# Cross attention on one core: an earlier x load, six warm-up products instead of 14, a last product in two halves, and a new order at both ends

## The chip, the cores and the metric

The kernel runs on one core of one Trainium2 chip. The metric is the device time of one execution in microseconds (us), the median of several runs. Beside it there is the trace of one execution, taken by the hardware profiler. Its engines are PE (TensorE matmuls; PEld are its weight loads), DVE (VectorE), ACT (ScalarE), POOL (GpSimd) and SP (SyncE, which here only issues DMA transfers).

## The reference

x has shape (2, 2048, 640), the text (2, 128, 384). The last four text rows (`ca`) are treated apart from the first 124 (`enc`). Cut to what matters, with eight heads of 80:

```python
enc, ca = text[:, :124, :], text[:, 124:, :]
hs = mha(x @ Wq, enc @ Wk, enc @ Wv)              # x attends to the text
ca_q1 = einsum('btc,th->bch', ca, Wq_ca)[:, indices, :]   # 2048 rows out of 384
ca_hs1 = mha(ca_q1, x, x)                         # the four rows attend to x
ca_hs2 = mha(ca_hs1 @ Wq, ca @ Wk_ca, ca @ Wv_ca)
out = (hs + ca_hs2) @ Wout + b_out + x
```

`mha` is softmax(q k^T / sqrt(80)) v for each head. All of it is float32.

## The kernel before, in words

The kernel is a set of generators, each of which hands out its steps one at a time. Every step names its engine, the steps it comes after, the rooms (PSUM banks, buffers) it takes and frees, and the marks it sets. `Desk.run` walks through the table `ORDER`. Each entry is the number of a task, whose next step is issued there; a letter behind it chooses ACT (`a`), DVE (`v`) or POOL (`g`) where a step may run on several engines. What is issued is pinned, so that each engine works strictly in the order of the table. The tile framework adds the waits. All DMA transfers that matter here are issued by SP, in the table's order, and a transfer waits for the one eight places ahead of it, since there are eight DMA semaphores.

The work is done in three stretches.

- **The front.** `first_loads` fetches four tiles of 128 rows of x (`xz`, one for each `row(k)`) and Wq in five chunks of rows (`wq_rows(c)`, into `wq_sb`), then Wq_ca, the text (`ctx_sb`), Wk_ca (`w_kca`), Wk (`w_k`) and further x rows (`xi`). `idle_work` multiplies a tile of zeros with itself (PSUM tile `unread`, helper `warm`); nothing reads the result. `x_first` transposes the first rows of x (`pt_x_0` to `pt_x_4`); `context` transposes the text (`pt_ctx_0` to `pt_ctx_2`), from which `ctxT`, `caT` and `cadT` are copied. `queries` forms the first queries (`pq_first`) chunk by chunk of x's columns, as chunks of Wq arrive. `y_weights` multiplies `w_kca` with `cadT` (`p2_kca`; the profile prints `p_kca`), and makes from it and from a turned Wq (`wq_turned`, `pt_wq_c_0` and `pt_wq_c_4`, c = 0 to 4) the weights `wyz` of the products `pyz`. `keys` makes `pk`, `text_values` the values `pv_b_u` of the two texts (24 matrix multiplies of 320 columns on the trace for a pair `b_u`).
- **The middle.** For 16 units of two tiles of 128 rows: queries (`pq`), scores against the text (`sc`), exponentials (`p`), products with values (`ph`, evacuated to `hs`), and for the four text rows the scores against x (`s1_...`, four multiplies of 512 columns into one PSUM tile of 2048), the maximum of each (`mx`, on DVE) and their exponentials. The tiles `s1_...` share PSUM room, so that a later one waits for the `mx` of an earlier one.
- **The end.** `text_out_fast` makes the output product `hs @ Wout` of a unit in seven products on sums and differences of blocks, whose partial results DVE adds in halves of 320 columns to x's rows, already in `x_more` or `last_rows`. The chains of partial products are run by `sums_chain`, with `po_m_...` the PSUM tile of unit m (`HALF` is 320). `stored` issues the store of a finished piece; in unit 15 a piece is half a row tile of 128, 128x320.

On PE the helper `matmul` cuts a product with 128 columns of weights into four strips of 32, each with its own weight load, so that a product is one row of the order and several rows of the trace. The profile's lines L211, L215, L219, L226 and L236 are the helpers for products, zeros, transposes, engine operations and transfers.

Of the kernel before, what the change touches and what calls it, by code (L numbers as in the profile page):

```python
# [66 lines left out]
class Desk:  # L67
# [7 lines left out]
        2 2 2 2 2 2 36 0 0 0 4 4 0 0 0 0 0 0 0 0 4 0 0 111a 6 6 6 0 4 6 4 2 2 2 2 2 2 2 4 113a 107 108 109 110 4 6  # L75
        114a 115a 3 6 3a 3 116v 4 6 3a 3 3v 6 3 8 8 7 7 7 2 15 15 15 11 15 15 12 8 7 0 0 118a 8 5 15 15 15 15 10 7
        117a 15 7 8 7 7 7 120a 9 1 119v 8 6 121a 7 7 7 7 122a 7 7 124v 9 123v 125a 126a 8 8 127 8 9 8 36 5 128 8 8 8 5
        9 9 9 129 5 130 15 36 15 15 131 9 9 14 14 9 14 14 14 14 9 14 6 112 136a 133a 135v 134v 14g 137 36 112 11 112
        15 14 15 36 14 12 14g 36 138 138 138 36 138 138 12 12 12 36 144v 145v 12 36 36 11a 9 9 9 139 11 9 9 9 140 143a
        9 146a 12 13 101 17 106 140 140 140 140 141 18 6 140 140 140 140 142 106 132 132 16 17 147g 148g 132 101v 142  # L80
        132 101v 101g 101g 101g 39 152 152 152 152 152 152 151 17 17 36 36 156a 142 142 142 18 18 18 18 18 18 18 18
        132 142 16 151 152 36 36 142 16 16 157a 43 151 152g 149g 152 16 132 16 101v 101 18 16 16g 36 159 159 16 36 158
        36 101g 150g 101g 17 160a 159 159 16 151 161a 16g 155 18 18 18 152 162 36 153 36 18 158 158 18 158 155 17 155
        153 36 20 20 19 163 159 159 163 163 21 21 171 163 142 142 158 172 164 163 163 36 21 21 172 172 172 172 21 43
        154 36 154 175 175 165 159 36 175 175 175 175 19 19 19 159g 166g 167g 159 36 36 170 39 181a 36 170 21 21 21 21
        172 172 172 19 20 19 19 182 177 176 177 182 175 19g 19 177 177 159 173 36 20 183a 170 20 36 168g 182 182 182
        182 172 19 184a 20 178 170 178 182 169g 175g 17 21 21 21 21 21 21 22 19g 177 174 177 185 23 182g 36 36 185 185
        186a 185 185 175 24 24 24 24 24 175 24 174 174 24 24 188 24 174 187 185 36 22 47 22 22 22 192 22 180 194 179
        36 180 192 192 192 192 22 192 22g 182 190 174 182 36 179 180 36 195 192 196 36 47 174 174 174 158 20 23 202 23
        23 24 24 24 197 22 197 198g 192g 199v 36 192 36 24 201g 24 206a 197 197 197 22 200g 197 23 202 23 208 51 207a  # L90
        208 174 189 208 208 208 208 197 197g 22g 36 209 209 36 202 205 209 214a 209 192 132 197 189 158 189 189 189
        197 132 189 202 36 215a 209 205 189 209 36 216 55 36 203 205 209 217 217 24 209g 36 26 26 217 217 217 217 209
        217 27 27 27 27 27 158 209 210 27 212 27 204 36 204 203 218 51 36 36 225 224 219g 220g 222g 221g 217g 36 193
        226 226 223 228 230a 223 228 36 226 226 226 226 232a 229 193 217 132 158 217 158 189 23 189 191 191 191 191 27
        55 231v 36 36 233v 229 223 226 193 193 193 234 234 226g 36 226 235 234 234 234 234 25 26 229 234 36 236 36 36
        27 191 226 191 191 191 191 27 211 36 227 223 227 237 27 238 234g 234 25 59 239 239 25 25 27 27 27 27 239 239
        239 239 36 211 36 211 132 211 211 177 36 26 59 26 36g 241 241 211 211 211 211 213 29 29 241 241 241 247 239
        243v 240 251v 25 36 36 36 26 244g 247 36 252 252 254a 36 247 36 252 252 30 234 213 56 177 30 30 30 30 213 213
        213 25 239g 241 241 239 239 240 177 245g 241g 242 249 36 36 252 253 252 255a 253 247 249 253 253 36 253 36 25
        256v 253 36 63 252 193 252 252 40 213 28 252 36 44 30 30 30 30 193 262 262 257 246g 240 241 250 263 241 177 25  # L100
        240 213 262 262 262 262 36 67 36 36 252 213 240 30 30 30 264 30 264 30 250 252 250 36 30 262 265 262g 262 264
        264 213 36 252 252 31 252 29 31 36 252 264 264 31 36 67 36 31 193 193 258 260 193 262 259 259 10 259 36 60 26
        33 33 33 33 252 252 252 29 36 29 252 29 32 268 32 31 33 267 267 33 33 259 266 266 259 264 264g 269g 270g 264
        266 266 36 266 266 268 36 36 268 268 268 63 252 266 252 252 252 252 276 268 276 266v 267 31 33 264 267 274 273
        276 276 252 282a 36 36 36 252 273 36 283 283 284v 273 36 276 276 36 36 283 283 248 36 248 259 242 259 259 283
        283 271g 272v 276 31 242 285v 273 36 36 31 267 32 259 31 283 36 283 266 286 287v 33 31 283 28 36 31 28 28 36
        31v 252 28 283 281 71 36 283 276v 289 283 281 261 261 261 261 261 261 25 28 266 277 28 261 36 290 33 283 290
        288 33 36 281 283 290 290 36 290 290 33 291 33 276 33 33 32 36 75 28 25 276 25 36 261 283 28 35 35 68 283 283
        290 25v 292 292 290g 242 242 290 292 292 292 261 292 25 25 32 32 275 298 292 36 298 283 36 283 34 293v 294g
        25v 298 298 75 36 292g 298 298 301 295g 301 290 292 36 280 242 280 242 275 275 275 292 302 288 275 28 301 301  # L110
        301 301 28 28g 301 304 279 242 71 279 242 242 305 306 242 305 305 305 305 305 297 103 35 242 283 35 242 242
        283 283 307 288 242 102 275 68 296g 66 66 31 31 31g 36 36 275 275 275 299 68 68 28 11 310v 301v 307 35 242 64
        314 29 283 314 283 28 35 315 301 314 28g 316 283 48 283 283 309 317a 242 242 297 309 283 313 242 313 318a 313
        242 314 314 309 313 297 316 316 305 242 242 288 288 301 10 305g 32 316 278 278 278 316 313a 320a 308 297 308
        316 305 242 323 319 242 324 242 34 34 34 34 313 325 68 68 68 105 103 104 104 267 48 79 242 332 242 48 48 34 46
        46 278 34 321 34 278 305 332 311g 328g 330g 329g 68 68 335a 68 242 336a 331g 312g 339g 340g 333g 341g 338g 34
        102 105 40 38 38 34 48 48 40 48 278 68 288 337a 332 332 332 332 79 242 344 242 348 332 344 242 346 348 346 344
        344 242 242 345 344 242 344 344 348 278 348 34 348 278 278 348 52 332g 332 347 344 242 345 83 242 349 349 242
        349 349 349 349 345 345 349 347 48 242 352a 48 48 48 334g 359 34g 242 242 300 44 300 34 332 40 40 40 44 44 40
        300 44 44 44 351 288 300 300 349g 355g 349 349 288 42 240 240 42 34 354a 353a 356g 34g 357g 343g 358g 342g 242  # L120
        360 83 242 360 360 365 359 365 242 365 365 365 365 359 359 362 362 365 242 361 359 242 242 300 104 361 360 359
        242 40 359 40 44 242 359 365g 363g 40 367a 300 40 300 369a 368a 300 372g 365 373g 371a 87 348 242 380 380 44
        242 242 242 381a 44 384v 374v 380 382a 380 380 52 44 242 242 242 380 364g 385g 375g 376 376 378 377 387 378
        387 376 387 387 376 379 387 376 379 288 240 50 52 288 52 240 242 52 242 52 242 242v 242 366 240 365 52 50 377
        380 380g 348g 393g 392g 327 387 376 242 377 387 376 242 242 242 391 303 303 303 303 303 380 377 376 327 267
        387 327 327 380 267 391 52 52 242 391 391 242 52 52 327 391 60 327 396v 397v 403 303 303 386v 383v 403 399v
        400g 401v 242 398a 91 407 407 242 391 303 303 322 35 64 391 407 407 407 407 403 391 242 389 407 327 395 403
        403 403 242 242 242 391 322 327 267 322 267 322 322 327 402v 407g 407 407 391 403 404 242 389 403 242 91 64 60
        327 64 64 391 322 391 391 391 242 404 404 408 408 348 322 408 408 242 408 408 404 390 348 64 64 58 409 370 408
        390 242 242 95 411 411 388 388 408g 408 322 391 391 388 242 322 326 411 411 411 411 242 95 411 388 412 412 391  # L130
        391 391 64 414v 242 391 413 408 62 62 411g 411 411 64 412 412 242 412 412 405 242 242 417v 405 87 418 412 418
# [108 lines left out]
def kernel(  # L240
# [42 lines left out]

# [1877 lines left out]
```

## Time and profile before

| | |
|---|---|
| time, median of 3 runs | 565.43 us (565.28 to 566.68) |
| the profiled execution's own time | 563.94 us |
| its span in the trace | 562.1 us |
| PE busy | 554.3 us, 99% |
| DVE busy | 386.8 us, 69% |
| ACT busy | 265.5 us, 47% |
| POOL busy | 198.9 us, 35% |
| moved by DMA | 101.47 MB, mean 181 GB/s |
| PE on the chain that ended last | 92% |
| DVE on that chain | 6% |

The span runs from the first to the last instruction of the trace; 1.84 us of the execution's own time lie outside it. PE is busy in nearly the whole span, but busy is not the same as advancing: in the first microseconds each multiply takes about twice as long as later, and the multiplies of zeros count as busy. A row of the timeline gives the start of a group in us from the span's start, then its length, the engine, the line, the operation, the tiles, the shape and how many instructions it holds. Groups on PE overlap a little, since the end of a multiply is modelled; the distance from one row's start to the next row's is the better duration.

### The profile page before, as it was taken

Reading aid. Unit: us, or ns where it says so; the run is one execution under the profiler, and the core shown is the slowest. Engines: PE = TensorE matmul, PEld = TensorE weight load, DVE = VectorE, ACT = ScalarE, POOL = GpSimd, SP = SyncE. Lnnn points to the kernel's source line nnn. Section 1 sums busy time; section 2 is a strip of 40 time slices with the busy share of each in tenths; the row PEclk is TensorE's granted clock in tenths of the full one; section 3 lists DMA queues with packets and bytes.
Section 4 is the critical chain, followed back from the end, with each engine's and each line's share of the span. In section 5 each row is a group of like instructions: output and inputs, shape, how many; then the busy total and the mean of one; then the engine's idle time right before and its main releaser. Section 6 shows DMA issues by size and latency. Waiting matters only on the chain.

```text
span 562.1 us, 18792 instructions
## 1 busy us (share of the span) xinstructions
PE 554.3 (99%) x8064; PEld 313.9 (56%) x8064; DVE 386.8 (69%) x622; ACT 265.5 (47%) x732; POOL 198.9 (35%) x211
## 2 busy tenths in 40 slices
PE   9999999999999999999999999999999999999997
PEld 8564455556555655555465445455545666666664
DVE  1457999999996564579999998755635655555534
ACT  3123645445338898886525424589878130100100
POOL 7002625344424522013469364512330513321310
PEclk9999999999999999999999999999999999999999
DMA  8994859764877989456568795859853687688703
GB/s 263 241 173 127 168 114 162 165 158 142 175 194 157 182 250 180 130 168 175 172 134 254 214 235 134 243 160 256 254 161 111 179 188 190 153 255 231 210 24 141
DMA packets 151554, 101.47 MB, mean 181 GB/s; under 512 B 86476, under 2 KB 130012, under 8 KB 151472
## 3 DMA queue, kind: packets, MB, share of 16 engines
q1 hardware_dynamic: 150704, 99.88, 69.8%
q8 instruction: 63, 1.03, 0.8%
q0 software_dynamic: 768, 0.40, 0.4%
q14 instruction: 19, 0.16, 0.1%
HBM read 61.34 MB, written 38.90 MB: 178 GB/s over the span
## 4 chain that ended last, share of the span: by engine, by line
PE 92%; DVE 6%; issue 1%; ACT 1%; DVEq 0%; ACTq 0%
PE po L211 26%; PE pq L211 25%; PE acc L211 8%; PE sc L211 7%; PE s L211 7%; PE ph L211 7%; DVE mx L226 4%; PE pq_first L211 3%; PE pyz L211 3%; PE pk L211 1%; PE unread L215 1%; PE pv L211 1%; DVE m L226 1%; PE pt_wq L219 1%; PE pt_x L219 0%
## 5 line engine op out<-in xcount | busy, mean ns | idle before, releaser
L226 DVE TENSOR_REDUCE mx<-s 128x4 f32<-128x2048 f32 x48 | 109.3, 2277 | 2.9 <-PE s L211 2.7
L226 ACT ACTIVATE p<-sc,m 128x124 f32<-128x124 f32 x256 | 89.8, 374 | 32.9 <-DVE m L226 32.9
L226 ACT ACTIVATE ea<-s 128x2048 f32<-128x2048 f32 x48 | 90.4, 1884 | 25.6 <-PE s L211 25.4
L226 POOL TENSOR_TENSOR p<-p,r 128x992 f32<-128x992 f32 x28 | 52.0, 1858 | 133.1 <-DVE r L226 129.2
L211 PE MATMUL po<-wout_sums,hs 128*32 128x320 f32 (+1 forms) x1012 | 77.8, 433 | 0.5 <-DVE x_more L226 0.5
L211 PE MATMUL po<-wout_sb,hs 128*32 128x320 f32 x956 | 76.9, 433 | 0.0
L226 DVE TENSOR_TENSOR x_more<-x_more,po 128x320 f32<-128x320 f32 x72 | 33.7, 481 | 44.6 <-PE po L211 44.5
L226 ACT ACTIVATION_READ_ACCUMULATOR p<-sc,m 128x1 f32 x256 | 55.4, 216 | 0.0
L211 PE MATMUL pq<-xt,wq_sb 128*32 128x256 f32 x896 | 54.3, 381 | 0.6 <-DVE q L226 0.6
L211 PEld LDWEIGHTS po<-wout_sums,hs 128*32 128x32 f32 (+1 forms) x1012 | 37.6, 110 | 29.5 <-issue 1.4
L211 PEld LDWEIGHTS po<-wout_sb,hs 128*32 128x32 f32 x956 | 36.3, 111 | 27.5 <-issue 0.9
L211 PE MATMUL acc<-ea,y_sb 128*32 128x384 f32 (+2 forms) x768 | 50.4, 384 | 0.0
L226 DVE TENSOR_REDUCE m<-sc 128x4 f32<-128x496 f32 x64 | 40.8, 663 | 13.4 <-PE sc L211 13.4
L226 POOL TENSOR_TENSOR hs<-hs 128x256 f32<-128x256 f32 x35 | 27.6, 796 | 60.9 <-DVE hs L226 52.4
L211 PE MATMUL ph<-pT,vpad 128*32 128x256 f32 x768 | 46.7, 380 | 0.3 <-ACT p L226 0.3
L226 DVE STREAM_TRANSPOSE eb<-p 128x1024 f32<-128x1024 f32 x32 | 39.5, 1234 | 5.0 <-POOL p L226 3.2
L226 DVE TENSOR_TENSOR last_rows<-last_rows,po 128x320 f32<-128x320 f32 x56 | 26.2, 479 | 23.1 <-PE po L211 22.9
L211 PEld LDWEIGHTS pq<-xt,wq_sb 128*32 128x32 f32 x896 | 27.5, 110 | 22.9 <-issue 5.5
L226 ACT COPY hs<-ph 128x512 f32<-128x512 f32 (+1 forms) x23 | 12.2, 543 | 58.8 <-PE ph L211 58.6
L211 PE MATMUL pq<-xt,wq 128*32 128x512 f32 x320 | 38.8, 595 | 0.0
L211 PEld LDWEIGHTS sc<-kmain,q 64*128 64x128 f32 x512 | 31.9, 187 | 11.7 <-issue 8.2
L211 PE MATMUL sc<-kmain,q 64*128 64x124 f32 x512 | 37.6, 283 | 0.1
(197 smaller groups left out, 792.5 us busy)
## 6 DMA issues: line engine op xcount, KB each, us to landing
kept<-eb SPq DMA_DIRECT2D x32, 512.0 KB
pT<-kept SPq DMA_DIRECT2D x48, 256.0 KB
landing<-away SPq DMA_DIRECT2D x60, 128.0 KB
xi<-in_x_dram SPq DMA_DIRECT2D x28, 256.0 KB
x_more<-in_x_dram SPq DMA_DIRECT2D x18, 320.0 KB
out_dram<-x_more SPq DMA_DIRECT2D x18, 320.0 KB
last_rows<-in_x_dram SPq DMA_DIRECT2D x14, 320.0 KB
y<-yt SPq DMA_DIRECT2D x16, 256.0 KB
```

What stands on the lines that cost most here:

```text
L211: self.pin(self.nc.tensor.matmul(out[strip], lhsT[:, strip], rhs, **kw))
L215: self.pin(self.nc.tensor.matmul(out, zeros, zeros, start=True, stop=True))
L219: self.pin(self.nc.tensor.transpose(out, in_, ident))
L226: return lambda *args, **kw: self.pin(getattr(engine, what)(*args, **kw))
```

## The change

Four edits, and an order that goes with them.

1. `first_loads` issues the second tile of x ahead of Wq's first chunk.
2. `IDLE` goes from 14 products of zeros to 6. Before, nine came ahead of `pt_x_0`, three between `pt_x_0` and `pt_x_1` and two among the `pt_wq`. Now all six come ahead of `pt_x_0`, and the transposes of x come after the mark "zeros".
3. The last chain of unit 15, a product of 12 steps over 320 columns with one addition and one store, is made as two chains of 160 columns, each with its addition and its store.
4. `ORDER` is recorded anew. Of some 2,235 entries about the first 250 and the last 45 differ; between them only task numbers shift.

```diff
-    FAST, SPARE, IDLE = 1, 0, 14
+    FAST, SPARE, IDLE = 1, 0, 6
...
-        for op in (row(0), wq_rows(0), row(1), row(2), row(3)):
+        for op in (row(0), row(1), wq_rows(0), row(2), row(3)):
...
-            yield Do("PE", product, [] if n else [op.at], frees=[(banks, at)] if n == IDLE - 1 else [])
+            end = n == IDLE - 1
+            yield Do("PE", product, [] if n else [op.at], frees=[(banks, at)] if end else [], marks=["zeros"] if end else [])
...
-            op = yield Do("PE", turn, [("xrows", n)] if n < 4 else [("xlast", k) for k in range(4)], needs=[(banks, 1)])
+            op = yield Do("PE", turn, [("xrows", n), "zeros"] if n < 4 else [("xlast", k) for k in range(4)], needs=[(banks, 1)])
...
-        def sums_chain(m, n, steps):
+        def sums_chain(m, n, steps, c0=0, c1=HALF):
...
-                            to[:, :HALF], l, r, start=(k == 0 and c == 0), stop=(c == len(pairs) - 1),
+                            to[:, c0:c1], l, r[:, c0:c1], start=(k == 0 and c == 0), stop=(c == len(pairs) - 1),
...
         for n, steps in enumerate(chains):
-            yield Fork(sums_chain(m, n, steps))
+            if m < UNITS - 1 or n < 3:
+                yield Fork(sums_chain(m, n, steps))
+            else:
+                left["products"] += 1
+                yield Fork(sums_chain(m, n, steps, 0, HALF // 2))
+                yield Fork(sums_chain(m, n + 1, steps, HALF // 2, HALF))
...
+    spans = (0, HALF), (HALF, H), (0, H), (HALF, HALF + HALF // 2), (HALF + HALF // 2, H)
...
     ORDER = """
-        2 2 2 2 2 2 36 0 0 0 4 4 0 0 0 0 0 0 0 0 4 0 0 111a 6 6 6 0 4 6 4 2 2 2 2 2 2 2 4 113a 107 108 109 110 4 6
+        36 0 4 4 0 0 0 0 0 2 2 2 2 2 107 0 0 4 4 111v 112a 6 6 6 6 6 4 2 110 2 2 2 2 2 2 2 4 3 108 109 114v 4 1 3v 3
...
```

**PE, the front.** These rows of PE's order before stand from the second set of `pq_first` products over 512 columns (which needs Wq's third chunk, DMAHW0) to the transposes `pt_wq_1_0`; a name in brackets is the semaphore waited for.

```order
L211 MATMUL pq_first_0_197<-xt_0_0_179,wq_sb_98 128x512 [waits DMAHW0_49]
L211 MATMUL pq_first_1_198<-xt_0_0_179,wq_sb_98 128x512
L211 MATMUL pq_first_2_199<-xt_0_0_179,wq_sb_98 128x512
L211 MATMUL pq_first_3_200<-xt_0_0_179,wq_sb_98 128x512
L211 MATMUL p2_kca_284<-w_kca_226,cadT_124 32x160 [waits DMAHW7_49,DVE_49]
L211 MATMUL p2_kca_284<-w_kca_226,cadT_124 32x160 x11
L219 MATMUL pt_wq_0_0_300<-ident_69,wq_sb_98 128x128 [waits Activation_49]
L219 MATMUL pt_wq_0_0_300<-ident_69,wq_sb_98 128x128 x3
L219 MATMUL pt_wq_0_4_322<-ident_69,wq4_99 128x128 [waits DVE_49,PE_49]
L215 MATMUL unread_177<-zeros_158 128x128 x2
L219 MATMUL pt_wq_1_0_339<-ident_69,wq_sb_98 128x128 [waits DVE_49,PE_49]
L219 MATMUL pt_wq_1_0_339<-ident_69,wq_sb_98 128x128 x3
```

The same place after the change:

```order
L219 MATMUL pt_wq_0_0_283<-ident_69,wq_sb_98 128x128 x4
L211 MATMUL p2_kca_305<-w_kca_231,cadT_124 32x160 [waits DVE_49,DMAHW7_49,Activation_49,Pool_49]
L211 MATMUL p2_kca_305<-w_kca_231,cadT_124 32x160 x11
L219 MATMUL pt_wq_0_4_327<-ident_69,wq4_99 128x128 [waits Activation_49]
L219 MATMUL pt_wq_1_0_329<-ident_69,wq_sb_98 128x128 [waits PE_49]
L219 MATMUL pt_wq_1_0_329<-ident_69,wq_sb_98 128x128 x3
L211 MATMUL pq_first_0_200<-xt_0_0_171,wq_sb_98 128x512 [waits DMAHW0_49]
L211 MATMUL pq_first_1_201<-xt_0_0_171,wq_sb_98 128x512
L211 MATMUL pq_first_2_202<-xt_0_0_171,wq_sb_98 128x512
L211 MATMUL pq_first_3_203<-xt_0_0_171,wq_sb_98 128x512
```

`p2_kca`, which waits for the transfer of `w_kca` (DMAHW7), now stands ahead of that set of `pq_first`; the two products of zeros are gone from here.

**PE, the values and the first scores.** Before, the end of the front reads:

```order
L211 MATMUL pv_0_1_634<-w_v_315,ctxT_122 32x320 x12
L211 MATMUL pv_1_0_647<-w_v_315,ctxT_122 32x320 [waits DVE_49,PE_49]
L211 MATMUL pv_1_0_647<-w_v_315,ctxT_122 32x320 x11
L211 MATMUL s1_0_0_1_0_660<-zop_0_0_531,cop_153 128x512 [waits PE_49]
L211 MATMUL s1_0_0_1_0_660<-zop_0_0_531,cop_153 128x512 x3
L211 MATMUL pv_1_1_671<-w_v_315,ctxT_122 32x320 [waits DVE_49,PE_49]
L211 MATMUL pv_1_1_671<-w_v_315,ctxT_122 32x320 x11
L211 MATMUL s1_0_0_1_1_685<-zop_0_0_531,cop_153 128x512 [waits DVE_49]
L211 MATMUL s1_0_0_1_1_685<-zop_0_0_531,cop_153 128x512 x3
```

After the change:

```order
L211 MATMUL pv_0_1_618<-w_v_301,ctxT_122 32x320 x12
L211 MATMUL s1_0_0_1_0_651<-zop_0_0_522,cop_153 128x512 [waits DVE_49]
L211 MATMUL s1_0_0_1_0_651<-zop_0_0_522,cop_153 128x512 x3
L211 MATMUL pv_1_0_657<-w_v_301,ctxT_122 32x320 x12
L211 MATMUL pv_1_1_670<-w_v_301,ctxT_122 32x320 [waits PE_49,Activation_49]
L211 MATMUL pv_1_1_670<-w_v_301,ctxT_122 32x320 x11
L211 MATMUL s1_0_0_1_1_683<-zop_0_0_522,cop_153 128x512 [waits DVE_49]
L211 MATMUL s1_0_0_1_1_683<-zop_0_0_522,cop_153 128x512 x3
```

`s1_0_0_1_0` moved ahead of `pv_1_0`, so that two sets of value products lie between it and `s1_0_0_1_1` instead of one.

More of the change, by code (lines that the diff above doesn't have):

```diff
@@ L80 @@
[L80 to L99, printed above, removed]
@@ L2086, in stored @@
         t, i, _ = xr_of[m][k]
-        cols = slice(0, H) if u == 2 else slice(u * HALF, (u + 1) * HALF)
+        cols = slice(*spans[u])
         yield Do(
```

150 lines of the change are left out of this document (88 added, 62 removed).

## The prediction

> **What bounds the kernel now.** I read the page first, for the engine that fills the span, and PE's waits next.
>
> ```profile
> span 562.1 us, 18792 instructions
> PE 554.3 (99%) x8064; PEld 313.9 (56%) x8064; DVE 386.8 (69%) x622; ACT 265.5 (47%) x732; POOL 198.9 (35%) x211
> PE s L211 <- DVE mx L226: 1.1, 2, 0.8
> ```
>
> PE is busy for 99% of the span, so time goes only with PE's work, its speed or its few waits. The wait to look at is `s` behind `mx`, once for 0.8 us. The change leaves the middle's order alone; what it does there is to pass on an earlier or later front. So I read the timeline of PE over the front, group by group.
>
> ```profile
> 1.13 4.21 PE L215 MATMUL unread<-zeros 128*128 128x128 f32 x18 [1.13 <-DVE zeros L226]
> 5.13 1.06 PE L219 MATMUL pt_x<-ident,xz 128*128 128x128 f32 x4
> 5.98 1.11 PE L215 MATMUL unread<-zeros 128*128 128x128 f32 x6
> 6.93 0.60 PE L219 MATMUL pt_x<-ident,xz 128*128 128x128 f32 x4
> 7.36 1.06 PE L211 MATMUL pq_first<-xt,wq_sb 128*128 128x128 f32 x8
> 8.26 1.04 PE L219 MATMUL pt_x<-ident,xz 128*128 128x128 f32 x8
> 9.13 0.60 PE L219 MATMUL pt_x<-ident,first_rows 128*128 128x128 f32 x4
> 9.57 1.06 PE L211 MATMUL pq_first<-xt,wq_sb 128*128 128x128 f32 x8
> 10.68 1.89 PE L211 MATMUL pq_first<-xt,wq_sb 128*128 128x256 f32 x8
> 12.62 3.60 PE L211 MATMUL pq_first<-xt,wq_sb 128*128 128x512 f32 x8
> 16.28 3.60 PE L211 MATMUL pq_first<-xt,wq_sb 128*128 128x512 f32 x8
> 19.81 1.02 PE L211 MATMUL p_kca<-w_kca,cadT 128*32 128x160 f32 x24
> 20.76 0.66 PE L219 MATMUL pt_wq<-ident,wq_sb 128*128 128x128 f32 x4
> 21.25 0.27 PE L219 MATMUL pt_wq<-ident,wq 128*128 128x128 f32 x1
> 21.36 0.61 PE L215 MATMUL unread<-zeros 128*128 128x128 f32 x4
> 21.81 0.60 PE L219 MATMUL pt_wq<-ident,wq_sb 128*128 128x128 f32 x4
> 27.71 1.52 PE L211 MATMUL pk<-ctxT,k 128*128 128x248 f32 x6
> 37.75 2.15 PE L211 MATMUL pyz<-xt,wyz 64*32 64x512 f32 x20
> ```
>
> From 1.13 us on PE never stands still here. But zeros fill some of it, and the start runs at half speed: four transposes take 0.85 us at 5.13 and 0.43 us at 6.93. What else could bound the front are the loads. DVE's timeline shows when they land, where DVE waited for them:
>
> ```profile
> 6.33 0.41 DVE L226 COPY first_rows<-xz 128x96 f32<-128x96 f32 x3 [1.88 <-DMA xz<-in_x_dram]
> 8.25 0.41 DVE L226 COPY first_rows<-xz 128x96 f32<-128x96 f32 x3 [0.39 <-DMA xz<-in_x_dram]
> 17.14 0.17 DVE L226 TENSOR_TENSOR cadT<-ctxT 128x18 f32<-128x18 f32 x1
> 17.47 0.88 DVE L226 COPY wq<-wq_sb 128x320 f32<-128x320 f32 x2 [0.17 <-DMA w_kca<-in_L_xattn_Wk_ca_dram]
> 22.20 0.59 DVE L226 COPY k<-w_k 128x192 f32<-128x192 f32 x2
> ```
>
> The third load, the second x tile, is there at 6.33, the fifth, the last x tile, at 8.25. Their order is what the change touches; the bytes ahead of the sixth load stay the same.
>
> **Part 1, loads and zeros.** Row and Wq chunk change places, so both are there by 6.33, when the first `pq_first` set can start. Before, it started at 7.36: a gain of 1.03 us, but only up to the next wait. Of the 14 products of zeros the twelve at 1.13 and 5.98 run beside that wait for loads, and only the last two, 21.36 to 21.81, cost 0.45 us that comes back. That the transposes now wait for all zeros costs nothing: six products are 12 of the 18 instructions of the first row, 12 x 4.00 / 18 = 2.67 us, done at 3.80, about when the first x tile can be used (by 5.13 at the latest).
>
> **Part 2, `p2_kca` ahead of a set of `pq_first`.** This is the term that decides. Up to `p2_kca` PE now has, at the distances of the rows: 0.90 and 1.11 us for two sets of 128 columns (the second with a text transpose), 0.87 and 0.44 for three transposes of x, 12.62 - 10.68 = 1.94, 16.28 - 12.62 = 3.66, and 0.49 for four `pt_wq` (20.76 to 21.25): 9.41 us. From 6.35 that gives 15.8; with a part of it at half speed about 16.1. There PE must wait for `w_kca` (and `cadT`). When that transfer lands is seen only from both sides. Not earlier than about 17.3: `cadT` is done then, and the change puts DVE's copies of Wq ahead of it, so that it won't be sooner; and a wait that ended at 17.47 is credited to this load. Not later than 19.81, where `p_kca` starts without a wait, nor, by the load of the same size behind it, much later than 19.7:
>
> ```profile
> w_kca<-in_L_xattn_Wk_ca_dram SPq DMA_DIRECT2D x1, 960.0 KB
> w_k<-in_L_xattn_Wk_dram SPq DMA_DIRECT2D x1, 960.0 KB
> 17.00:18.00 1.00, 1.00 (x4) 0.38 (x2) 0.79 (x4) 0.00 (x0) 0.00 (x0) 1.00 1.03 387
> ```
>
> `w_k` is in use at 22.20 without a wait; 983,040 bytes at the 387 GB/s of that microsecond are 2.5 us. I take 18.0, half a us behind the row that names the load, since its parts on the DMA engines need not end together. So PE stands still for about 1.9 us. From `p2_kca` at 18.06 the work to `pyz` is that of before, 37.75 - 19.81 = 17.94, less the zeros 0.45, less the four `pt_wq` already done 0.49, plus the set of `pq_first` that is now behind, 19.81 - 16.28 = 3.53: 20.53, and `pyz` starts at 38.6, **0.84 us later** than before. With the load at 17.3 it is 0.14 us later, at 19.7 it is 2.5 us later. The other loads have room: four `xi` transfers go ahead of `w_k`, but `w_k` is wanted only for the `pk` at 27.71, 7.9 us behind `p2_kca`.
>
> **Part 3, the first scores.** Here are PE's and DVE's timelines at the end of the front, and the load on which the `sc` behind it rest.
>
> ```profile
> 49.52 5.08 PE L211 MATMUL pv<-w_v,ctxT 128*32 128x320 f32 x72
> 54.53 0.50 PE L211 MATMUL s<-zop,cop 32*128 32x512 f32 x4
> 54.96 1.82 PE L211 MATMUL pv<-w_v,ctxT 128*32 128x320 f32 x24
> 57.60 0.51 PE L211 MATMUL s<-zop,cop 32*128 32x512 f32 x4 [0.82 <-DVE mx L226]
> 63.41 0.50 PE L211 MATMUL s<-zop,cop 32*128 32x512 f32 x4
> 55.26 2.28 DVE L226 TENSOR_REDUCE mx<-s 128x4 f32<-128x2048 f32 x1
> 60.98 2.28 DVE L226 TENSOR_REDUCE mx<-s 128x4 f32<-128x2048 f32 x1
> 58.44 1.14 ACT L226 CAST rests<-first_rests 128x512 fp32r<-128x512 f32 x2 [0.99 <-DMA away<-first_rests]
> ```
>
> Between the two `s` there were 24 instructions of `pv`, 1.82 us, against an `mx` of 2.28 that began 0.3 us after its `s` had ended: PE waited 0.82 us. Now 48 instructions lie there, 48 x 5.01 / 72 = 3.34 us, which covers an `mx` and the gap: the wait goes, **-0.82 us**. Late next would be `s1_0_0_2_0` at 63.41, behind the `mx` that runs from 60.98 to 63.26: 0.15 us of room. If DVE comes there later by the copies that were moved, up to 0.5 us comes back; DVE's row before 60.98 was waiting for PE's `sc`, so I take 0. The two terms leave 0.84 - 0.82 = **+0.02 us** for the whole middle.
>
> **Part 4, the end.** The chain's last piece, and DVE's and SP's last rows:
>
> ```profile
> 535.28 23.17 PE po L211 x344
> 558.47 0.49 DVE L226 TENSOR_TENSOR last_rows<-last_rows,po 128x320 f32<-128x320 f32 x1 [1.13 <-PE po L211]
> 557.37 1.95 SPq L236 DMA_DIRECT2D out_dram<-last_rows  x3
> ```
>
> PE runs without a gap, at 23.17 / 344 = 67 ns for an instruction; the last product's 24 take 1.62 us. Two halves of 24 instructions with 160 columns cost between 1.62 (half of 67 ns each) and 1.90 (the `p_kca` row, of the same width: 20.76 - 19.81 = 0.95 a half). I take +0.14. The first half's addition and store lie beside the second half's product of 0.9 us. What is left behind the last product: an addition of 160 columns instead of 320, between half of 0.49 and all of it, I take -0.16; and a store of 80 KB instead of 160 KB, 0 to -0.3 us out of the 2.8 us from SP's last issue (559.3) to the end, I take -0.1. Together **-0.1 us**. The new order of the last 45 steps moves `po` products past each other; each waits for DVE's additions, and one wait more would cost up to 0.5 us, as large as one addition. I take 0.
>
> **The sum.** +0.84 - 0.82 - 0.12 = -0.1 us: 563.94 becomes 563.8 in the profiled execution. The median of before, 565.43, lies 1.5 us above its profiled execution, and the same shift gives **565.3 us**. A measurement of this kernel tells 0.3%, 1.7 us, from no change.
>
> **Rival A, the load comes late (slower).** `w_kca` lands at 19.7 and not at 18.0, and PE, which had the set of `pq_first` to do meanwhile, stands still for 3.6 us. It costs +2.5 - 0.82 - 0.1 = +1.6 us: 567.0. It decides from a landing at 18.1, where the sum is zero. For it: DMA is at full share there (1.03), and `w_k`, in use at 22.20, excludes nothing below 19.7. Against: the wait at 17.47. Chance 0.12.
>
> **Rival B, the clock (slower).** Half speed ends between 5.98 and 6.93, as said, after more than five us without a gap. Now PE has gaps before 6.35, while it waits for the second x tile and Wq. If half speed lasts 3.4 us more, it doubles up to 1.7 us of work; the 1.9 us of waiting for `w_kca` takes that up: no cost. With 6.8 us, 3.4 - 1.9 = +1.5 us, 566.8. If the standstill itself brings half speed back for 3.4 us, nothing takes it up: +1.7 us, 567.0. The Trainium skill, TensorE: Matmul & The Clock Gate, Part 1: The HAM clock gate, says that the clock is released after a busy window of about 3.4 us, that the window runs freely, and that an idle window of that length throttles it again; it thus speaks against taking zeros away. The trace agrees in the first point (released after 5.4 us of work at most); no gap in it is long enough to show the last. By that rule a gap of 1.9 us alone does not bring half speed back. Chance of a cost 0.15.
>
> **Rival C, the load comes early (faster).** At 17.3 the sum is -0.8 us; with a store and an addition at their best -1.1, 564.3. More is not to be had there: `rests` at 58.44 waits for a transfer, and `sc` for `rests`, so a PE much ahead of before would wait at 59. Chance 0.13, and only with a gain from all terms together would it pass 0.3%.
>
> **How the numbers follow.** The forecast (a net within 0.7 us of zero) has 0.60, A 0.12, B 0.15, C 0.13. Faster by over 0.3%, below 563.7: half of C, and a little from the spread of the runs, 0.08. Slower, above 567.1: about half of A and B and a little of the forecast, 0.17. The rest, 0.75, is the same. The range goes from C's 564.3, with 0.3 us for the runs' spread, 564.0, to A and B at 567.0 and 0.2 us more, 567.2.
>
> **What would show it.** Right: `p_kca` starts near 18.0 behind a PE gap of 1.5 to 2.3 us with DMA as releaser; `pyz` starts near 38.6; the `s` behind the second pair of `pv` has no wait and starts within 0.3 us of 57.6; `po` ends 0.1 us later than the middle's shift says, and the tail behind it is 0.2 to 0.3 us shorter. Wrong: a `p_kca` at 19 or later (A), transposes of 0.2 us each after 8 us or `po` steps doubled anywhere behind the gap (B), a new wait of `s` behind `mx` at 63 us, or a wait among the last `po`.

## The result and the profile after

The changed kernel took 567.64 us, median of 22 runs (564.01 to 574.6), the kernel before 565.49 us, median of 22 (564.1 to 567.91). The ratio, with disturbed runs left out, is 1.0033, 95% interval 1.0018 to 1.0049. So it is 0.33% slower, where 565.3 us and no change were forecast, and 567.64 lies 0.4 us above the range's upper end. The execution profiled first took 569.08 us, 1.4 us above the median; two more profiles of the same kernel, `after_again` (565.33 us) and `after_third` (568.83 us), are used beside it.

PE's timeline of the changed kernel (first profile) over the front:

```profile
5.91 2.02 PE L211 MATMUL pq_first<-xt,wq_sb 128*128 128x128 f32 x16
...
19.18 1.78 PE L211 MATMUL p_kca<-w_kca,cadT 128*32 128x160 f32 x24 [3.08 <-DMA w_kca<-in_L_xattn_Wk_ca_dram]
...
21.16 1.06 PE L219 MATMUL pt_wq<-ident,wq_sb 128*128 128x128 f32 x4
...
41.25 2.15 PE L211 MATMUL pyz<-xt,wyz 64*32 64x512 f32 x20
...
57.00 3.44 PE L211 MATMUL pv<-w_v,ctxT 128*32 128x320 f32 x48
60.37 0.50 PE L211 MATMUL s<-zop,cop 32*128 32x512 f32 x4
```

PE stands still for 3.08 us in front of `p_kca`, until `w_kca` is there. What follows runs at half speed, which is called a fall of the clock below: the row of `p_kca` lasts 1.78 us, where it was 1.02 before, and that of four `pt_wq` 1.06, where it was 0.60. The wait of the `s` behind the second pair of `pv` for `mx` is gone (60.37). The view of stretches shows the clock: after each stretch's length stand the busy times of PE, PEld, DVE, ACT and POOL with their counts, then the granted clock, the DMA share and GB/s.

```profile
15.88:19.29 3.41, 0.33 (x7) 0.14 (x8) 1.05 (x4) 0.58 (x1) 0.00 (x0) 1.00 1.25 191
19.29:22.71 3.42, 3.42 (x30) 2.58 (x30) 0.91 (x4) 0.27 (x1) 0.00 (x0) 0.50 0.95 128
```

PE's timeline of `after_again`, where the standstill was short, and the stretch that holds it:

```profile
17.67 1.02 PE L211 MATMUL p_kca<-w_kca,cadT 128*32 128x160 f32 x24 [1.40 <-DMA w_kca<-in_L_xattn_Wk_ca_dram]
...
38.12 2.15 PE L211 MATMUL pyz<-xt,wyz 64*32 64x512 f32 x20
...
57.68 1.16 PE L211 MATMUL sc<-kmain,q 64*128 64x124 f32 x16
...
63.15 0.51 PE L211 MATMUL s<-zop,cop 32*128 32x512 f32 x4 [0.29 <-DVE mx L226]
...
73.02 1.92 PE L211 MATMUL pq<-xt,wq 128*32 128x512 f32 x16
```

```profile
16.37:19.78 3.41, 2.11 (x31) 1.65 (x32) 0.81 (x4) 0.79 (x2) 0.00 (x0) 1.00 0.88 99
```

And the two views of `after_third`:

```profile
18.08 1.02 PE L211 MATMUL p_kca<-w_kca,cadT 128*32 128x160 f32 x24 [1.86 <-DMA w_kca<-in_L_xattn_Wk_ca_dram]
...
40.22 2.15 PE L211 MATMUL pyz<-xt,wyz 64*32 64x512 f32 x20
```

```profile
15.77:19.19 3.42, 1.56 (x30) 1.10 (x28) 0.61 (x5) 0.59 (x1) 0.00 (x0) 1.00 1.12 170
19.19:22.60 3.41, 3.41 (x8) 1.88 (x8) 1.60 (x6) 0.27 (x1) 0.00 (x0) 0.50 0.78 104
```

The clock fell behind the standstill in two traces of three, with 0.33 and 1.56 us of work in the window of the wait, and held in the third, with 2.11. From the start of `p_kca` to that of `pyz` it took 22.07 us (41.25 - 19.18) and 22.14 (40.22 - 18.08), against 20.45 (38.12 - 17.67) where the clock held: one fall costs 1.6 to 1.7 us.

The second loss lies behind the front, and no part of the prediction speaks of it. Here is SP's timeline of the kernel before, then that of the changed kernel (first profile), at the transfers `landing`, which bring the rests of queries for the next `sc`:

```profile
59.05 0.33 SPq L236 DMA_DIRECT2D landing<-away  x1
...
59.98 1.62 SPq L236 DMA_DIRECT2D landing<-away  x3
...
61.65 10.43 SPq L236 DMA_DIRECT2D xi<-in_x_dram  x9
```

```profile
63.06 0.66 SPq L236 DMA_DIRECT2D xi<-in_x_dram  x1
63.81 2.94 SPq L236 DMA_DIRECT2D landing<-away  x4
```

An `xi` load now stands ahead of the four `landing`. ACT, which must cast what lands before it makes `yz`, before and after:

```profile
64.61 0.62 ACT L226 CAST rests<-landing 128x512 fp32r<-128x512 f32 x1 [0.74 <-DMA landing<-away]
```

```profile
70.55 0.62 ACT L226 CAST rests<-landing 128x512 fp32r<-128x512 f32 x1 [4.19 <-DMA landing<-away]
```

And PE, from the first `sc` of the program to a `pq` behind the second, before and after:

```profile
58.04 1.16 PE L211 MATMUL sc<-kmain,q 64*128 64x124 f32 x16
...
72.02 1.92 PE L211 MATMUL pq<-xt,wq 128*32 128x512 f32 x16
```

```profile
60.80 1.16 PE L211 MATMUL sc<-kmain,q 64*128 64x124 f32 x16
...
71.81 1.51 PE L211 MATMUL sc<-kmain,q 64*128 64x124 f32 x14 [0.55 <-ACT yz L226]
...
76.16 1.92 PE L211 MATMUL pq<-xt,wq 128*32 128x512 f32 x16
```

From the first of these rows to the last PE does the same work. It takes 13.98 us before (72.02 - 58.04) and 15.36 after (76.16 - 60.80): PE waits 0.55 us for `yz`, with which ACT is late, and the `sc` behind it go in pieces. In `after_again` and `after_third` it takes 15.34 and 15.25 us, with ACT's wait at 4.26 and 4.12. These 1.3 to 1.4 us are in all three traces of the changed kernel.

The end of the changed kernel, PE and DVE:

```profile
562.28 0.76 PE L211 MATMUL po<-wout_sb,hs 128*32 128x160 f32 x16
...
563.09 0.76 PE L211 MATMUL po<-wout_sb,hs 128*32 128x160 f32 x16
...
564.17 0.32 DVE L226 TENSOR_TENSOR last_rows<-last_rows,po 128x160 f32<-128x160 f32 x1 [0.49 <-PE po L211]
```

A half takes 0.81 us from start to start, two of them 1.62, what the whole product took by 24 instructions of 67 ns. From the end of the last addition to that of the span it is 2.9 us (564.49 to 567.4), 3.1 us before (558.96 to 562.1). From the start of PE's last row of `s` to the end of the span it is 128.4 us in the kernel before (433.67 to 562.1) and 128.0 in all three traces of the changed kernel (in the first, 439.35 to 567.4): the new end saves 0.4 us.

Between the two ends the traces differ without any change of the order. From PE's row of `s` at 176.91 us of the kernel before to that last row the orders are the same, and it takes 256.8 us in the kernel before and 257.8 to 259.3 in the three traces of the changed kernel, but also 258.5 in `end_only`, an experiment below whose order is that of before up to the end. So a difference of 2 us between two spans is not yet one of the kernels.

### The profile page after: what moved, and what is told of

It reads as the page before. It is cut to its first block, busy times and chain, and to the rows that moved or that the text cites. A ratio compares the mean times of both kernels' runs of the same rounds, so it can differ in the third digit from the quotient of the medians.

```text
span 567.4 us, 18817 instructions
## 1 busy us (share of the span) xinstructions
PE 555.2 (98%) x8072; PEld 313.4 (55%) x8072; DVE 389.7 (69%) x624; ACT 263.7 (46%) x730; POOL 199.4 (35%) x212
## 4 chain that ended last, share of the span: by engine, by line
PE 79%; DVE 8%; DMA 6%; SPq 4%; issue 2%; ACT 1%; DVEq 0%; ACTq 0%
PE po L211 26%; PE pq L211 20%; PE ph L211 7%; PE acc L211 7%; PE sc L211 6%; PE s L211 6%; SPq L236 4%; DVE mx L226 3%; PE pyz L211 2%; PE pq_first L211 2%; DMA w_kca<-in_L_xattn_Wk_ca_dram 2%; DVE m L226 1%; PE pk L211 1%; DMA wq_sb<-in_L_xattn_Wq_dram 1%; DMA xi<-in_x_dram 1%
## 5 line engine op out<-in xcount | busy, mean ns | idle before, releaser
L211 PE MATMUL po<-wout_sb,hs 128*32 128x320 f32 (+2 forms) x972 | 77.4, 429 | 0.0
L211 PEld LDWEIGHTS po<-wout_sb,hs 128*32 128x32 f32 (+1 forms) x972 | 36.7, 111 | 27.4 <-issue 0.9
L226 DVE TENSOR_TENSOR last_rows<-last_rows,po 128x320 f32<-128x320 f32 (+1 forms) x57 | 26.4, 472 | 23.9 <-PE po L211 23.7
## 6 DMA issues: line engine op xcount, KB each, us to landing
landing<-away SPq DMA_DIRECT2D x60, 128.0 KB
```

The costliest lines, as they stand in the source:

```text
L211: self.pin(self.nc.tensor.matmul(out[strip], lhsT[:, strip], rhs, **kw))
L226: return lambda *args, **kw: self.pin(getattr(engine, what)(*args, **kw))
```

## The experiments

All ratios are to the kernel before, run on the same chip, with 95% intervals. A "run with a fall" is one whose mean granted clock was under 0.9985; one window of 3.41 us at half speed makes 0.997 of a run. The kernel before had 8 of 113 in the batches of the experiments (3 of 33 in the first of them). The changed kernel had 6 of the 19 that the ratio uses (their median 568.0 us, that of the 13 others 566.4) and 9 of all its 22. Numbers in the diffs are entries of the order's table.

**The place of `p2_kca` undone** (`pkca_behind`). One entry, a set of `pq_first`, goes back in front of it.

```diff
-  10 8 11 117a 8 7 7 7 6 7
+  10 6 8 11 117a 8 7 7 7 7
```

> The changed kernel with one entry of the table moved: the set of pq_first that needs Wq's third chunk stands ahead of p2_kca again, as before. Theory (the standstill in front of p2_kca is the loss, and it also lets the clock fall): PE works 3.5 us of its own through the wait for w_kca, p_kca starts within 0.5 us of the load's landing or of 19.4 us, no half-speed window follows, pyz starts at 36 to 37.5 us instead of 41.25, and the median is 2 to 4 us below the changed kernel's 567.64, near 564.5. Rival (the loss lies in the transfers' new order and in the middle): pyz starts earlier all the same, but PE waits the gained time at 60 to 76 us for the transfers, and the median stays above 566.5.

Ratio 1.0034 (1.0013 to 1.0054), median 567.77: nothing won that can be told. PE's timeline:

```profile
19.73 1.02 PE L211 MATMUL p_kca<-w_kca,cadT 128*32 128x160 f32 x24
...
57.58 1.16 PE L211 MATMUL sc<-kmain,q 64*128 64x124 f32 x16
...
68.75 1.51 PE L211 MATMUL sc<-kmain,q 64*128 64x124 f32 x14 [0.82 <-ACT yz L226]
...
73.11 1.92 PE L211 MATMUL pq<-xt,wq 128*32 128x512 f32 x16
```

The standstill is gone, and the first `sc` starts 3.2 us sooner than in the changed kernel's first profile and 0.46 us sooner than before (58.04). But from there to the `pq` it takes 15.53 us, 1.55 more than before. By these rows PE is 1.1 us later than before, which is 0.19% and lies in the interval. So the theory that the standstill is the main loss fell, and the rival, that the gained time is lost again at 60 to 76 us, held. Three of 11 runs had a fall, so the clock falls without that standstill too.

**The standstill filled with zeros** (`zeros_in_gap`).

```diff
                     pt = bank(s[0], f"pt_wq_{i}_{c0}")
+                    for _ in range(8 if (i, c0) == (0, 0) else 0):
+                        desk.warm(pt[:, :P], zeros_of[0])
```

> The changed kernel with eight products of zeros more, written into the tile pt_wq_0_0 ahead of its transposes, so that PE works about 1.8 us of the 3.1 us in which it stood still; p2_kca keeps its place and its wait. Theory that the stillness lets the clock fall: p_kca starts at the same time as in the changed kernel (18 to 19.2), but takes 0.95 us and not 1.7, no window at half speed is seen behind it in any run (granted clock 0.999 to 1.000 in all), and the runs at 0.991 to 0.997 with their 568 to 574 us are gone: median 1 to 1.7 us lower, near 566.3. Rival, that the half-speed windows come from elsewhere: clocks of 0.997 in about 9 of 22 runs as before, median unchanged at 567.6.

Ratio 1.0050 (1.0026 to 1.0073), median 567.95. In the trace 0.46 us of the standstill is left, and the row of `p_kca` is 1.02 again. But the clock falls 50 us later, behind the wait for `yz`. PE's timeline and two stretches:

```profile
18.58 1.02 PE L211 MATMUL p_kca<-w_kca,cadT 128*32 128x160 f32 x24 [0.46 <-DMA w_kca<-in_L_xattn_Wk_ca_dram]
```

```profile
67.48:70.89 3.41, 1.95 (x28) 0.86 (x20) 1.17 (x4) 1.87 (x4) 0.27 (x1) 1.00 0.95 111
70.89:74.31 3.42, 3.42 (x30) 2.99 (x34) 3.41 (x5) 1.00 (x2) 2.34 (x3) 0.50 1.10 156
```

Three of 10 runs had a fall. The zeros did not lower the median.

**The `xi` load behind `landing`** (`landing_first`). One entry 18, an `xi` load, is moved behind the 146, which are the `landing`.

```diff
-  142 142 142 142 106 18 17 101g 101v 101g 147g 148g 146
-  146 101g 39 152 152 36 146 146 146 18 18 18 18 18 18 18
+  142 142 142 142 106 17 101g 101v 101g 147g 148g 146 146
+  101g 39 152 152 36 146 146 146 18 18 18 18 18 18 18 18
```

> The changed kernel with one entry moved: the first xi load of the next x tiles (256 KB) is issued behind the four landing transfers and not ahead of them. Theory that this load holds up landing, and with it the rests on ACT, yz and sc: landing has arrived about 1.5 to 2 us sooner, the 4.2 us of ACT's wait for it shrink to about 2, the wait of sc for yz (0.5 us) and the slow first sc go, and PE's lag against the kernel before grows by 0 to 0.2 us instead of 1.2 us between the s at 60 and the pq at 74; median about 1 us lower than the changed kernel's, 566.6. Rival, that landing is late only because the front is late: nothing changes, 567.6.

Ratio 1.0002 (0.9985 to 1.0019), median 565.66: nothing is left of the loss that can be told. The timelines of SP, ACT and PE:

```profile
61.18 2.19 SPq L236 DMA_DIRECT2D landing<-away  x4
...
66.45 0.62 ACT L226 CAST rests<-landing 128x512 fp32r<-128x512 f32 x1 [2.00 <-DMA landing<-away]
...
58.93 1.16 PE L211 MATMUL sc<-kmain,q 64*128 64x124 f32 x16
...
73.07 1.92 PE L211 MATMUL pq<-xt,wq 128*32 128x512 f32 x16
```

ACT waits 2.0 us instead of 4.2, and from `sc` to `pq` it takes 14.14 us instead of 15.36. This theory held in its mechanism. By the ratios the move was worth 0.31%, 1.8 us; with their intervals that does not differ from the 1.2 us of the trace. Five of 12 runs had a fall; a fall alone is therefore not what the ratio of the changed kernel shows. In this trace the fall does not stand behind `w_kca` at all, but behind a wait for a chunk of Wq (`wq_sb`). PE's timeline and two stretches:

```profile
6.99 3.32 PE L211 MATMUL pq_first<-xt,wq_sb 128*128 128x128 f32 x16 [1.50 <-DMA wq_sb<-in_L_xattn_Wq_dram]
```

```profile
4.05:7.46 3.41, 1.65 (x13) 1.20 (x12) 1.08 (x3) 0.58 (x1) 3.40 (x18) 1.00 0.87 278
7.46:10.88 3.42, 3.42 (x18) 3.42 (x18) 1.04 (x9) 0.00 (x0) 3.42 (x7) 0.50 1.04 400
```

**Both moves**, by the two diffs above (`landing_and_pkca`).

> The changed kernel with both entries moved: the set of pq_first ahead of p2_kca, and the xi load behind the four landing transfers. Theory (two losses in a row: the standstill for w_kca, and the landing transfers behind the xi load, where the second takes whatever is saved at the first): with both gone the median falls by more than with landing_first alone (565.66), to 563 to 564.5, below the kernel before, and PE's wait of sc for yz is under 0.3 us. Rival (a third limit at 55 to 70 us, the chain from the first rests through away and landing): no better than landing_first, 565 to 566.

Ratio 1.0002 (0.9985 to 1.0019), median 565.08. Beside `pkca_behind` that is again 0.32% from the `xi` load's place. Beside `landing_first`, the place of `p2_kca` brings 0.6 us in the median and nothing in the ratio, with a fall in one run of 12 instead of five. It is level with the kernel before; the theory, which had it below that at 563 to 564.5 us, fell.

**The `xi` load ahead of `landing` in the kernel before** (`before_xi_ahead`).

```diff
-  132 101v 142 132 101v 101g 101g 101g
+  132 101v 18 142 132 101v 101g 101g 101g
-  156a 142 142 142 18 18 18 18 18 18 18 18
+  156a 142 142 142 18 18 18 18 18 18 18
```

> The kernel before with one entry of its table moved: the first xi load of the next x tiles ahead of the four landing transfers, as in the changed kernel. Theory that this place alone costs most of the loss: landing arrives 1.5 to 2.5 us later than the 64.5 us of before, ACT waits 2.5 us or more for it at 61 to 68 us and not 0.7, sc waits for yz, and the median rises by 1 to 2 us over 565.07. Rival, that before has room for it because its landing transfers stood otherwise between the y transfers: less than 0.5 us.

```profile
68.18 0.62 ACT L226 CAST rests<-landing 128x512 fp32r<-128x512 f32 x1 [4.19 <-DMA landing<-away]
...
58.04 1.16 PE L211 MATMUL sc<-kmain,q 64*128 64x124 f32 x16
...
73.79 1.92 PE L211 MATMUL pq<-xt,wq 128*32 128x512 f32 x16
```

The timelines of ACT and PE show the changed kernel's wait of 4.19 us and 15.75 us from `sc` to `pq`, 1.8 more than before, and that run took 567.08 us. But the ratio is 0.9999 (0.9978 to 1.0020), the median 565.0: over its runs the load's place costs the kernel before nothing that can be told, and the theory that this place alone costs most of the loss fell. Of the 3.2 us by which this run's span is longer than that of before, 1.8 lie here and 1.6 between 177 us and the last `s`, where the orders are the same. Why the other runs are not longer is not settled.

**The second half of the rests sooner** (`rests_first`): its steps on ACT and DVE go ahead of both `mx`, as before the change.

```diff
-  11 139a 36 36 36 12 12 36 138 140a 9 138 144v 143a
+  11 138 139a 138 36 36 36 12 12 36 140a 9 146v 145a
```

> The changed kernel with two entries moved: ACT's and DVE's second half of first_rests (a copy and an addition) ahead of the two mx, as before, and not behind them; the order of PE and of the transfers stays. Theory (landing comes late because the second half of first_rests stands behind the mx that part 3 of the change pulled ahead: at 59.3 us and not at 52.2, so that away, which carries it, is issued 5 us later and landing with it): away is issued before 57 us, landing has arrived by 67 us, ACT waits less than 2 us for it, the sc behind yz loses no time, and the median falls by 1.2 to 2 us under the changed kernel's 567.64, to 565.6 to 566.4. Rival (the xi load ahead of landing is enough by itself): landing still last at 69 us or later, median above 567.

The timelines of SP and ACT, and two stretches:

```profile
56.94 0.55 SPq L236 DMA_DIRECT2D away<-first_rests  x1
...
62.95 3.18 SPq L236 DMA_DIRECT2D landing<-away  x4
...
70.55 0.62 ACT L226 CAST rests<-landing 128x512 fp32r<-128x512 f32 x1 [4.79 <-DMA landing<-away]
```

```profile
69.58:72.99 3.41, 2.17 (x28) 1.23 (x22) 1.39 (x5) 2.44 (x5) 0.00 (x0) 1.00 0.90 120
72.99:76.40 3.41, 3.41 (x36) 2.38 (x38) 3.41 (x5) 0.44 (x1) 2.90 (x3) 0.50 1.29 144
```

`away`, which feeds `landing`, goes out at 56.94, but `landing` is still issued behind the `xi` load, at 62.95, and ACT waits 4.79 us. The clock falls behind PE's wait for it. Ratio 1.0050 (1.0027 to 1.0072), with a fall in 8 of 12 runs: this theory fell. What is late is the place of `landing` on SP, not what feeds it.

**One part at a time on the kernel before.** The end alone (`end_only`): the table's last two rows, the product in two spans of columns, and `stored` with them, on the old front.

```diff
-            yield Fork(sums_chain(m, n, steps))
+            if m < UNITS - 1 or n < 3:
+                yield Fork(sums_chain(m, n, steps))
+            else:
+                left["products"] += 1
+                yield Fork(sums_chain(m, n, steps, 0, HALF // 2))
+                yield Fork(sums_chain(m, n + 1, steps, HALF // 2, HALF))
```

> The kernel before with the end of the changed one alone: the last 45 entries of its table, and the last product, addition and store in halves; the front, the loads and the 14 zeros are those of before. By the prediction's part 4: 0.1 us faster than before (0.14 more on PE, 0.16 and 0.1 less behind it), ratio 0.9998. Rival, a wait among the reordered last products: 0.5 us slower, ratio 1.001.

Ratio 0.9997 (0.9982 to 1.0011), as forecast and within what can be told from nothing. In its trace it takes 128.0 us from the last row of `s` to the end (435.77 to 563.8), as in the changed kernel.

Six zeros and the x row's load alone (`six_zeros`), with eight entries 0 taken out of the table:

```diff
-    FAST, SPARE, IDLE = 1, 0, 14
+    FAST, SPARE, IDLE = 1, 0, 6
-        for op in (row(0), wq_rows(0), row(1), row(2), row(3)):
+        for op in (row(0), row(1), wq_rows(0), row(2), row(3)):
```

> The kernel before with part 1 alone: the second x tile loaded ahead of Wq's first chunk and six products of zeros instead of 14, with the rest of its order. Theory of the prediction: the first pq_first starts at 5.9 to 6.4 us instead of 7.36 and 0.45 us more goes at 21 us; p2_kca, then reached at about 18.3 us, has no wait; pyz starts 1 to 1.5 us earlier; 0.8 to 1.5 us faster if the rests and landing transfers follow, else 0 to 0.5. Rival, the clock: with PE idle between 4 and 6 us the half-speed stretch lasts a window of 3.4 us longer or comes again, PE loses up to 1.7 us between 6 and 13 us, and the median is 0.3 to 1.5 us above before.

Ratio 1.0004 (0.9989 to 1.0018). The front gained less than expected: `pyz` starts at 37.60 us, 0.15 ahead of before, where 1 to 1.5 were forecast. The first `pq_first` does start at 6.14 instead of 7.36, but PE then waits 0.57 and 0.22 us for the next tiles of x. Later it waits for the rests, and the clock falls behind that wait. PE's timeline and two stretches:

```profile
59.69 0.78 PE L211 MATMUL sc<-krest,rests 64*128 64x124 f32 x8 [0.65 <-ACT rests L226]
```

```profile
56.68:60.09 3.41, 2.00 (x28) 1.56 (x28) 2.56 (x5) 1.62 (x5) 0.25 (x2) 1.00 0.46 147
60.09:63.50 3.41, 3.41 (x38) 1.69 (x40) 3.00 (x3) 2.35 (x14) 3.19 (x3) 0.50 0.75 212
```

That wait is not PE's lead: ACT starts on the rests at 59.02, 0.58 us later than before (58.44).

The early `s1_0_0_1_0` with its `mx` alone (`scores_early`):

```diff
-  138 138 12 12 12 36 144v 145v 12 36 36 11a
+  138 138 12 12 36 36 12 144v 145v 12 36 11a
```

> The kernel before with s1_0_0_1_0 ahead of pv_1_0 and its mx ahead of the copies of pv_0_1 and pv_1_0, as the change has it. Part 3 of the prediction alone: the 0.82 us wait of s for mx goes, the next s at 63.4 us keeps its start less 0.8; 0.8 us faster, ratio 0.9986. Rival: the time is given back at the next mx, at sc for rests (the cast on ACT at 58.4 waits for a transfer) or at landing; within 0.2 us of before.

Ratio 1.0005 (0.9993 to 1.0017), where 0.9986 was forecast: the rival, that the time is given back, held. The wait for `mx` became a longer one of `pv`, for a copy that now stands behind that `mx` on DVE:

```profile
56.70 1.82 PE L211 MATMUL pv<-w_v,ctxT 128*32 128x320 f32 x24 [1.26 <-DVE vpad L226]
```

**The changed kernel twice more**, unchanged (`after_again`, `after_third`), for their traces, which are read above.

> The changed kernel once more, for a second trace, since its first lies 1.4 us above its median. If the losses are the order's own, p_kca waits for w_kca again (1.5 us or more), landing arrives 5 us or more later than in before, and ACT waits 3 us or more for it, with sc behind yz. If they were accidents of the first trace, one of these is gone.

> The changed kernel a third time, same question. Both theories say that the half-speed windows differ from run to run: the windows run freely against the start of the program, so that the 3 us standstill fills one window in some runs and falls into two in others.

Both waits, for `w_kca` and for `landing`, are there in both.

**The standstill filled, and `xi` behind `landing`**, by the two diffs above (`landing_zeros`).

> The changed kernel with the xi load behind landing, as in landing_first, and eight products of zeros in the standstill in front of p2_kca, as in zeros_in_gap. If the standstill lets the clock fall, the granted clock is 0.999 or more in at least 11 of 12 runs (landing_first: 7 of 12), and the median is 565.2 to 565.5, that of landing_first's runs at full clock. If the windows at half speed come from elsewhere, 3 to 6 of 12 runs show 0.997 or less, as without the zeros.

Ratio 1.0023 (1.0004 to 1.0042), median 566.04, with a fall in two of 12 runs. The falls are fewer than the five of `landing_first`, yet the median is not lower, and neither forecast was met. What the falls cost in the median is not settled by this. Beside `zeros_in_gap`, which differs by the place of the `xi` load alone, the ratio is 0.27% lower.

**A version from these moves.** `tuned` has both moves of `landing_and_pkca`, the early rests, the last 2 (the load of `w_k`) ahead of the `xi` rows (15), an 8 (`fold`) sooner and the 1 (the sums of masks) later; `tuned2` is the same without the early rests. Beside `landing_and_pkca`:

```diff
-  108 109 114v 4 1 3v 3 115a 6 3a 3 116a 4 6 3v 7 7
-  7 3 8 15 15 15 15 2 15 15 15 15 12 15
+  108 109 114v 4 3v 3 115a 6 3a 3 116a 4 6 3v 1 7 7
+  7 3 8 2 15 15 15 15 15 15 15 15 12 15
-  7 7 7 7 119v 8 9
+  7 7 7 7 8 119v 9
```

> The changed kernel with all moves that the runs so far point to: pq_first ahead of p2_kca, the xi load behind landing, the second half of first_rests ahead of the mx, the loads of w_k ahead of the xi rows, and on DVE fold ahead of a copy of pt_wq and the small sums of masks behind the copies of Wq. Theory that these delays are what ate the gain: no wait of PE above 0.5 us before 70 us except the loads at 5 us and the 1.1 us at the start, PE at the s behind the values 0.5 to 1 us ahead of before, median 564 to 564.6, ratio 0.998 to 0.9995. Rival (the chain of transfers of the rests sets the time at 59 us in any order): ratio 0.9995 to 1.0005.

> The kernel tuned without its early first_rests: pq_first ahead of p2_kca, the xi load behind landing, w_k ahead of the xi rows, fold ahead of a copy of pt_wq, the sums of masks later. Theory that the second half of first_rests ahead of the mx does harm (rests_first was slower than the changed kernel, 568.3 to 567.6): 564 to 564.8, ratio to before 0.998 to 0.9990. Rival, that it makes no difference once the xi load is out of the way: 565.05 as tuned, ratio 0.9985 to 1.0000.

`tuned`: 0.9988 (0.9973 to 1.0004), median 565.05, where 564 to 564.6 was forecast. `tuned2`: 0.9986 (0.9971 to 1.0000), median 564.54 beside 565.01 of the kernel before, and no run of 12 with a fall. It has the lowest ratio here. Against the changed kernel's ratio that is 0.5% less; against the kernel before, 0.14%, with an interval that ends at 1.0000, less than can be told from no change. `tuned` and `tuned2` cannot be told apart.

## Why the prediction was wrong

**The step that failed** is the end of part 3: "The two terms leave 0.84 - 0.82 = +0.02 us for the whole middle". It followed PE and DVE up to 63 us and left out SP, though the new table moves a 256 KB `xi` load past four `landing` transfers. In the three traces of the changed kernel and that of `pkca_behind`, from the first `sc` to the `pq` it takes 15.25 to 15.53 us, in `landing_first` 14.14, with the load moved back: 1.1 to 1.4 us, where the step had 0.02. The other traces agree. Leaving out three with a fall on this stretch (`six_zeros`, `rests_first`, `zeros_in_gap`), the five with the load ahead (these four and `before_xi_ahead`) take 15.25 to 15.75 us, the eight with the load behind 13.81 to 14.42. Three pairs of kernels that differ in this place alone (the changed kernel and `landing_first`, `pkca_behind` and `landing_and_pkca`, `zeros_in_gap` and `landing_zeros`) differ by 0.31, 0.32 and 0.27% in their ratios; one such pair lies at the edge of its intervals, but all three go the same way. That the same place cost the kernel before nothing over its runs speaks against it as a cause in every order; in the changed order it is shown.

**Rival B** was priced rightly for one fall; that its chance was too low is what the traces say, not the ratios, since `pkca_behind` and `zeros_in_gap`, which take the standstill away or fill it, won nothing. The standstill brought half speed back in two traces of three, at 1.6 to 1.7 us (forecast 1.7), where the whole of B had 0.15. That it could come of a wait of 1.9 us was argued away by the rule of the Trainium skill, TensorE: Matmul & The Clock Gate, Part 1: The HAM clock gate, that an idle window of about 3.4 us throttles the clock. `after_third` disagrees: its wait was 1.86 us, PE was busy for 1.56 us of the window's 3.42, and the next window ran at 0.50. **Rival A's** sign, a `p_kca` at 19 or later, came in the first trace (19.18, behind 3.08 us) and not in the other two: when `w_kca` lands differs by 1.5 us from run to run.

**Part 1** had the first `pq_first` at 6.33; it starts at 5.91, 6.61 and 6.27 in the three traces. But that both loads are there by then is not sure: PE waited for `wq_sb` in the second and third of them, and in `landing_first` until 6.99, with a fall behind it. **Part 2** was right without the clock: `p_kca` at 17.67 to 19.18 (18.06), a standstill of 1.4 to 3.1 us (1.9), `pyz` at 38.12 where the clock held (38.6). With the clock down it was 40.22 and 41.25, which only rival B had. **Part 3's** wait did go in the changed kernel, from 3.44 us of `pv` between the two `s` (3.34 said); the wait for `mx` at 63 us was taken at 0; in `after_again` it is 0.29 us and in the other two there is none. That this gain needs more of the new order than the scores' place, `scores_early` shows. **Part 4** was right in direction and too small: the end saves 0.4 us in the traces, 0.12 said. The halves cost nothing more on PE (0 instead of +0.14), the last addition is 0.17 us shorter (0.16 said) and what lies behind it 0.2 (0.1 said). **Rival C's** bound, a wait for the rests at 59 us for a PE much ahead, is not shown: in `six_zeros` the rests themselves came later, and in `tuned2` PE reached the first `sc` at 57.41, 0.63 us ahead of before, and did not wait for them.

Ahead of the failed step the sum held in the one trace of the changed kernel without a fall: in `after_again` the first `sc` stands 0.36 us ahead of before (57.68 against 58.04), where the net of parts 2 and 3 had said +0.02. As an estimate, 1.3 us at `landing` and 1.7 us in 6 of 19 runs instead of 8 of 113, 0.4 us, make 1.7 us; the ratio says 1.9. But the end's 0.4 us the other way and the front's own gain are not in this, so that the two figures lie close in part by luck.

**What stays open:** what part of the ratio each of the two is, since the intervals are 0.3 to 0.4% wide and the traces of one order lie 2 us and more apart; why zeros in the standstill did not help; and why the load's place cost the kernel before nothing over its runs.

## What to carry to other kernels

When an order changes, write down for each queue, the one that issues transfers too, what has moved past what, and follow the receiver of each transfer that was overtaken: here, in the changed order, one load moved back behind four smaller ones won back as much as had been lost. Ask of a new wait not only how long it is, but what the window of the clock that holds it still has of work: a wait of 1.9 us cost another 1.7, and one of 1.4 us cost nothing more. And a gain at one load is worth only what the next loads leave of it: in `six_zeros` 1.22 us at the first `pq_first` were 0.15 at `pyz`.

## What the runs showed of the hardware

The granted clock fell behind windows that were only partly idle. It changed at distances of whole windows of 3.41 us: in the first profile of the changed kernel it rose at 5.64 us, fell at 19.29, four windows later, and rose again at 22.71, one later. Half speed followed windows in which PE was busy for 0.33 us (`after`), 1.56 (`after_third`), 1.65 (`landing_first`), 1.95 (`zeros_in_gap`), 2.00 (`six_zeros`) and 2.17 (`rests_first`). It didn't follow one with 2.11 (`after_again`), one with 1.76 (`before_xi_ahead`, from 306.37 us) and two in a row with 1.86 and 2.17 (`rests_first`, from 14.96 us), in which a wait of 2.79 us for `w_kca` lies. So busy time alone doesn't draw the edge: between 1.5 and 2.2 us of 3.41 it went either way. In `zeros_in_gap` half speed lasted two windows, 70.89 to 77.72 us, and the run's mean clock was 0.994.
